# A sandwich layer on one core: attention's small products in halves over two steps, and in another order

## The chip, the cores and the metric

The kernel runs on one core of one Trainium2 chip. The metric is the device time of one execution in microseconds. Before the change it is 2101.61 us, the median of three runs (2100.98 to 2102.13). The profile is one more execution; it took 2102.66 us, of which 2100.9 us lie between its first and its last instruction (the span).

The engines are named as in the profile: PE (matrix products, with PEld for the weight loads that run beside them), DVE (VectorE), ACT (ScalarE), POOL (GpSimd) and SP, which only issues transfers. Each takes its instructions in the order in which the program issues them.

## What is computed

The input x has 8 batches of 512 rows and 512 columns, float32. Two sublayers follow each other, each as x + layernorm(f(layernorm(x))).

```python
# attention, 16 heads of 32 columns; every column is rotated (SPLIT is 0)
c_kv = x @ W_dkv + b_dkv                      # 128 columns
v = c_kv @ W_uv + b_uv
c_q = x @ W_dq + b_dq                         # 128 columns
q = rotary(c_q @ W_qr + b_qr)
k = rotary(x @ W_kr + b_kr)
out = softmax(q @ k.T / sqrt(32)) @ v         # by head
out = out @ W_o + b_o
# feed-forward: two Walsh-Hadamard transforms around a gated layer of 2048
x = fwht(x * SU_ug) / 64
x = silu(x @ W_gate.T * s_g) * (x @ W_up.T * s_u)
x = (fwht(x * SU_dp) / 64) @ W_down.T * s_d
```

The kernel moves the second transform into the down weights: it transforms W_down once, in 16 portions of 32 columns, while attention runs (a "fold"), and writes them to DRAM for the feed-forward part.

## The kernel before

**Steps.** Attention is a loop of 128 steps. Step t belongs to group n = t // 4 and key block c = t % 4; a group is four heads of one batch, so a batch b has 16 steps, i = 0 to 15. What the engines do in a step is written out by hand, in this order:

- `scores_t(n, c)` (L564, L573): transposed scores of one key block of 128 keys for four heads, with the row maximum brought in as a bias by four bf16 products (L564); these mark the start of a step in the trace. ACT exponentiates them in two instructions (L585), the first at once, the second after `bias_rows` where a group ends (c = 3).
- `turn()`: issues pending rotations. A rotation is a DVE shuffle (L420) and three POOL instructions (L421 to L423) which read and overwrite the tile `lin`; `lin` has three buffers.
- `invert` (c = 0), `divide` (c = 3): softmax sums and the quotient.
- `weigh` (L606): probabilities times values, of the key block of the step before.
- `bias_rows(n + 1)` (L550) at c = 3: transposes the row maxima of the next group, which POOL's `split` (L543 to L545) has cut into three bf16 parts.
- `add_up` (L594) at c = 1 and c = 3: four POOL additions that bring two key blocks together. At c = 0 of the next group DVE adds the two pairs (`add_pairs`, L599); `sums` (L623) at c = 2 needs that one.
- a "between" piece, `weighed`, and `row_max` (L527) for the group six steps ahead: scores of 128 queries for four heads, whose maxima DVE takes in two reductions (L535). At c = 1 `split` follows.
- `early`: layer norm and residual instructions on ACT and POOL; a second `turn()`; `later`: statistics, loads and stores; one DVE level of a fold (L493, L494).
- a "behind" piece.

**Pieces.** The projections of the next batch, folds, output projections and input transposes are pieces of work put between these steps by two tables, `BETWEEN` and `BEHIND`, indexed by i. A piece is one to nine products into a PSUM tile of 512 columns and an eviction by ACT: `key` and `compress` four products (3.63 us on PE), `out_proj` five, `query`, `value` and `fold` one (about 1.06 us).

**PSUM.** All pieces, `bias_rows` and `sums` use one bank, `ps_f`, with one buffer. `scores_t` and `row_max` use the three buffers of `ps_s`, four tiles a step: so the second `row_max` tile of a step waits for the first exponential of that step, and the second score tile of the next step waits for a reduction. `wide` puts a piece into `ps_s` instead, so that it may stand next to a piece in `ps_f` (the steps `TWO`).

**Loads and ends.** `load_x` brings the x of the batch after next (1 MB) at i = 4, `x_stats` at i = 6 to 9, `x_norm` at 12, 14, 15 and 0. In the last batch `ENTRY` places the first steps of the feed-forward input (`in_step`) at fixed places. The feed-forward part follows attention and isn't touched.

Of the kernel before, what the change touches and what calls it, by code (L numbers as in the profile page):

```python
# [10 lines left out]
F32 = mybir.dt.float32  # L11
BF16 = mybir.dt.bfloat16
I32 = mybir.dt.int32
AF = mybir.ActivationFunctionType
# [3 lines left out]
P = 128  # L18
NB, S, D = 8, 512, 512
DH, GH = 32, 4  # L20
NK = D // P
NT = S // P
# [11 lines left out]
def sandwich_kernel(  # L34
# [142 lines left out]
    def in_step(j, had, n):  # L177

        if had:
            in_had(j)  # L180
            if j + 2 < n:
                in_shift(j + 2)
            return
        in_flip(j)
        if j + 3 < n:
            in_load(j + 3)
        if j + 1 < n:
            in_norm(j + 1)
        if j + 2 < n:
            in_stats(j + 2)  # L190
# [51 lines left out]
    with ExitStack() as actx:  # L242
# [19 lines left out]
        def load_x(b, by=1):  # L262
            xs[b] = xpool.tile([P, NT, D], F32, tag="x", name=f"x{b}")
            xv = x[b].rearrange("(c p) d -> p c d", p=P)
            for c in range(0, NT, by):
                nc.sync.dma_start(out=xs[b][:, c : c + by, :], in_=xv[:, c : c + by, :])

        def load_row(b, t):

            if b < NB - 1:  # L270
                xr[b, t] = row.tile([P, D], F32, tag="xr", name=f"xr_{b}_{t}", bufs=2)
            else:
                xr[b, t] = fo.tile(
                    [P, D], F32, tag="wwza"[t], name=f"xr_{b}_{t}", bufs=2 - t // 2
                )
            nc.sync.dma_start(out=xr[b, t], in_=x[b, ts(t, P), :])

# [100 lines left out]
        def x_shift(b):  # L378
            mv, rs = stats[b]
            stats[b] = rs, shift_of(mv, rs, NT, f"x{b}")  # L380

        def x_norm(b, t):
            rs, sh = stats[b]
            xn[b, t] = row.tile([P, D], F32, tag="xn", name=f"xn_{b}_{t}", bufs=3)
            nc.scalar.activation(
                xn[b, t], xs[b][:, t, :], AF.Identity, bias=sh[:, t : t + 1], scale=rs[:, t : t + 1]
            )
# [26 lines left out]
        def rotate(dst, ps, bias, scale, name, first=None, second=None):  # L414
            lin = rp.tile([P, S], F32, tag="lin", name=f"lin_{name}")
            nc.scalar.activation(lin, ps, AF.Identity, bias=bias, scale=scale)

            def rest():
                rot = rp.tile([P, S], F32, tag="rot", name=f"rot_{name}", bufs=2)
                nc.vector.stream_shuffle(rot, lin, swap)  # L420
                (first or nc.gpsimd).tensor_mul(lin, lin, cs[:, 0, :])  # L421
                (second or nc.gpsimd).tensor_mul(rot, rot, cs[:, 1, :])
                (first or nc.gpsimd).tensor_add(dst, lin, rot)  # L423

            turns.append(rest)

        turns = []

        def turn():

            while turns:
                turns.pop(0)()

        def key(b, g, wide=False):
            if g == 0:
# [43 lines left out]
            )  # L479
            folds.append((n, w))  # L480

        def fold(n, wide=False):
            _, w = folds.pop(0)
            ps = bank(wide, f"fd_{n}").rearrange("p (c m) -> p c m", c=NI)
            nc.tensor.matmul(ps, lhsT=h128, rhs=w, start=True, stop=True)
            z = fo.tile([P, NI, NF], F32, tag="z", name=f"fz_{n}")
            a = fo.tile([P, NI, NF], F32, tag="a", name=f"fa_{n}")
            nc.scalar.copy(z, ps)

            def level(src, dst, h):  # L490
                sv = src.rearrange("p (a t b) n -> p a t (b n)", t=2, b=h)
                dv = dst.rearrange("p (a t b) n -> p a t (b n)", t=2, b=h)
                nc.vector.tensor_add(dv[:, :, 0, :], sv[:, :, 0, :], sv[:, :, 1, :])  # L493
                nc.vector.tensor_sub(dv[:, :, 1, :], sv[:, :, 0, :], sv[:, :, 1, :])  # L494

            def keep():
                nc.sync.dma_start(
                    out=wdd.rearrange("p (c m) -> p c m", c=NI)[:, :, ts(n, NF)], in_=w
                )

            levels.extend(
                [
                    lambda: level(z, a, 1),
                    lambda: level(a, z, 2),
                    lambda: level(z, a, 4),
                    lambda: level(a, w, 8),
                    keep,
                ]
            )

        levels = []


        brow, nms, pt, o_ps, o_sb, rec = {}, {}, {}, {}, {}, {}
# [245 lines left out]
        for t in range(3):  # L760
# [10 lines left out]

        BETWEEN = {
            0: (x_flip, 1, 1), 1: (x_flip, 1, 2), 4: (x_flip, 1, 3),
            8: (query, 1, 0), 9: (query, 1, 1), 12: (query, 1, 2), 13: (x_flip, 2, 0),
        }
        BEHIND = {
            0: (value, 0, 2), 1: (key, 0, 3), 2: (query, 0, 3), 3: (value, 0, 3),
            5: (compress, 1, "cq"), 6: (key, 1, 0), 7: (out_proj, -1, 0),  # L780
            8: (out_proj, -1, 1), 9: (out_proj, -1, 2), 10: (out_proj, -1, 3),
            11: (key, 1, 1), 12: (compress, 1, "ckv"), 13: (value, 1, 0), 14: (key, 1, 2),
            15: (value, 1, 1),
        }

        FIRST_BETWEEN = {i: p for i, p in BETWEEN.items() if i not in (8, 9)}
        FIRST_BEHIND = {
            **BEHIND, 7: (query, 1, 0), 8: (None, NB, None), 9: (key, 1, 1),
            10: (None, NB, None), 11: (query, 1, 1),
        }  # L790
        OUT = {7: 0, 8: 1, 9: 2, 10: 3}

        APART = {n: (0, 2) for n in range(NG - NK, NG - 2)}
        APART[NG - 2], APART[NG - 1] = (0, 2, 3), (0, 1, 2, 3)

        FOLDS = [4, 10, 15] + [NK * NT * b + i for b in range(1, NB - 1) for i in (4, 10)]
        FOLDS.append(NK * NT * (NB - 1) + 1)
        READ = [0] + [g - 3 for g in FOLDS[1:]]


        TWO = (8, 9, 10, 12, 15)

        def piece(table, b, i, wide=False):
            if b == 0 and table is BEHIND and i == 8:
                out_bias()
            pieces = table if b else FIRST_BETWEEN if table is BETWEEN else FIRST_BEHIND
            if i in pieces:
                fn, d, what = pieces[i]
                if 0 <= b + d < NB:
                    fn(b + d, what, *([True] if wide else []))  # L810
            at = NK * NT * b + i
            if at in FOLDS and (table is BETWEEN) == (b > 0 and i in TWO or i == 15 or b == NB - 1):
                fold(FOLDS.index(at), wide)
            if b == NB - 1 and (i, table is BEHIND) in ENTRY:
                in_step(*ENTRY[i, table is BEHIND], 2 * NT)

        places = [
            (0, False), (4, False), (4, True), (5, True), (6, True), (8, False), (10, False),  # L820
            (11, True), (12, False), (12, True), (13, True), (14, True), (15, True),
        ]
        ENTRY = {place: divmod(s, 2) for s, place in enumerate(places)}
        room["xin"] = lambda name: row.tile([P, D], F32, tag="xn", name=name, bufs=3)
# [9 lines left out]
        def early(b, i):  # L834

            if b > 0 and i - 3 in OUT:
                residual(b - 1, OUT[i - 3])
            if b + 2 < NB and i in (12, 14, 15):
                x_norm(b + 2, max(i - 13, 0))
            if i == 0 and 0 < b + 1 < NB:  # L840
                x_norm(b + 1, 3)

        def later(b, i):

            if b > 0 and i - 1 in OUT:
                out_stats(b - 1, OUT[i - 1])
            if b > 0 and i - 2 in OUT:
                out_shift(b - 1, OUT[i - 2])
            if b > 0 and i - 5 in OUT:
                store(b - 1, OUT[i - 5])  # L850
            if b + 2 < NB:
                if i == 4:
                    load_x(b + 2, NT)
                elif 6 <= i < 10:
                    x_stats(b + 2, i - 6)
                elif i == 11:
                    x_shift(b + 2)

        for t in range(NG * NT):
            n, c = divmod(t, NT)  # L860
# [4 lines left out]
            ends_group = c == NT - 1 and n + 1 < NG  # L865
            if not ends_group:
                second()
            turn()
            if c == 0 and n > 1:
                invert(n - 2)  # L870
            if c == 3 and n > 1:
                divide(n - 2)
            last_steps = t + AHEAD >= NG * NT
            if last_steps:
                piece(BETWEEN, b, i)
            if t > 0:
                weigh(*divmod(t - 1, NT))
            if ends_group:
# [6 lines left out]
                    sums(n - 1, APART[n - 1])  # L885
            elif c == 2 and n > 0:
                sums(n - 1)
            if not last_steps and (i not in TWO or b == NB - 1):
                piece(BETWEEN, b, i)
            if c == 0 and n > 0:  # L890
                weighed(n - 1)
            u = t + AHEAD
# [2 lines left out]
                if u % NT == NT - 1:  # L895
                    split(u // NT)
            early(b, i)
            turn()
            if c == 0 and 0 < n <= NG - NK:
                add_pairs(n - 1)  # L900
            later(b, i)
            if b == 0 and i == 6:
                out_bias_in()
            if levels and (c > 0 or 0 < i and b < 1):
                levels.pop(0)()
            if small:
                small.pop(0)()
            if t in READ:
                fold_load(READ.index(t))
# [14 lines left out]
                load_row(b, i - 12)  # L924
            elif b == NB - 1 and i in (8, 10):
                combine(*units[i // 2 - 4][1:])
            if i in TWO and b < NB - 1:
                piece(BETWEEN, b, i, True)
            piece(BEHIND, b, i)
            if n == NG - 1 and c == 2:  # L930
                invert(NG - 2)

# [682 lines left out]
```

## Time and profile before

| | |
|---|---|
| median of three runs | 2101.61 us |
| profiled execution | 2102.66 us, span 2100.9 us |
| before step 0 | 46.8 us |
| batch 0 | 102.1 us |
| batch 1 | 108.6 us |
| batches 2 to 5 | 108.7 us each |
| batch 6 | 108.1 us |
| batch 7, steps 0 to 12 | 81.6 us |
| from there to the end | 1219.0 us |

The times by batch are differences between the starts of L564 in the timeline. In 257.5 to 366.2 us (batch 2) PE is busy for 108.65 us, DVE 83.71, ACT 57.83 and POOL 90.53. PE's durations in the timeline have modelled ends and overlap; the starts are what is read here. The length of a piece of PE work is therefore the distance from its start to the start of the next one, and a wait shows as a distance that is larger than that of the same work elsewhere. A float32 product shows as two matmul records.

### The profile page before, as it was taken

How to read it: one execution, taken by the hardware profiler on the slowest of the kernel's cores; microseconds unless marked ns; L12 is line 12 of the kernel's file. 1: busy time of each engine (PE TensorE's matmuls, PEld its weight loads, DVE VectorE, ACT ScalarE, POOL GpSimd, SP SyncE). 2: the span in 40 equal slices, each digit the busy share in tenths (PEclk: the TensorE clock that was granted, in tenths of full speed). 3: DMA queues.
4: the chain of work that ended last, by engine and by line, in shares of the span. 5: the costliest groups of instructions: out<-in, count | busy, mean ns of one | idle time of the engine just before them, and what ended most of it. 6: DMA issues, size and time to landing. Idle time of an engine off the chain costs nothing.

```text
span 2100.9 us, 26741 instructions
## 1 busy us (share of the span) xinstructions
PE 2076.8 (99%) x9035; PEld 1057.4 (50%) x9042; DVE 1414.4 (67%) x2356; ACT 745.3 (35%) x1199; POOL 1575.4 (75%) x1629
## 2 busy tenths in 40 slices
PE   8999999999999999999999999999999999999998
PEld 4333333333333333344444677676676766777753
DVE  5698777676767677465545866678866678656542
ACT  3554545555555545522121122222222222222211
POOL 4787979787878889645453678788888879787852
PEclk9999999999999999999999999999999999999999
DMA  3112121212121122237454444444343344444432
GB/s 122 37 31 51 42 54 49 47 51 52 46 57 46 32 66 72 70 104 221 145 166 152 146 143 148 133 138 149 130 157 131 131 137 144 138 158 136 138 112 70
DMA packets 215913, 218.12 MB, mean 104 GB/s; under 512 B 87376, under 2 KB 147920, under 8 KB 215776
## 3 DMA queue, kind: packets, MB, share of 16 engines
q1 hardware_dynamic: 215424, 215.32, 33.2%
q8 instruction: 72, 1.18, 0.2%
q0 software_dynamic: 352, 1.08, 0.1%
q14 instruction: 65, 0.53, 0.1%
HBM read 169.18 MB, written 46.92 MB: 103 GB/s over the span
## 4 chain that ended last, share of the span: by engine, by line
PE 94%; DVE 3%; issue 1%; POOL 1%; ACT 1%; DMA 0%; SPq 0%; POOLq 0%; DVEq 0%; ACTq 0%
PE d L1123 24%; PE psy L1225 18%; PE s L527 6%; PE ops L606 6%; PE ps_k L439 5%; PE ps_y L662 5%; PE t L573 5%; PE u L1106 5%; PE g L1106 4%; PE psz L1516 3%; PE t L564 3%; PE l L623 2%; PE ps_q L454 2%; PE ps_v L466 1%; PE ps_cq L407 1%; PE fxh L207 1%
## 5 line engine op out<-in xcount | busy, mean ns | idle before, releaser
L1225 PE MATMUL psy<-wd,g 128*128 128x512 f32 x896 | 448.9, 592 | 0.0
L535 DVE TENSOR_REDUCE nm<-s 128x2 f32<-128x1024 f32 x256 | 300.8, 1216 | 175.1 <-PE s L527 175.1
L1347 POOL TENSOR_TENSOR pr<-pr,pr 128x512 f32<-128x512 f32 x294 | 391.6, 1357 | 9.0
L594 POOL TENSOR_TENSOR p<-p,p 128x512 f32<-128x512 f32 x244 | 330.2, 1384 | 22.1 <-PE ops L606 22.1
L585 ACT ACTIVATE p<-t 128x1024 f32<-128x1024 f32 x256 | 251.8, 1023 | 89.0 <-PE t L573 89.0
L1123 PE MATMUL d<-xb,wq 128*128 128x256 f32 x992 | 254.2, 380 | 1.9 <-DVE inner L1139 1.4
L1123 PEld LDWEIGHTS d<-tt,wq 128*128 128x128 f32 x864 | 164.0, 190 | 144.4 <-issue 106.0
L1123 PE MATMUL d<-tt,wq 128*128 128x256 f32 x864 | 233.8, 379 | 0.2 <-DVE pr L1144 0.2
L1140 POOL TENSOR_TENSOR pr<-inner 128x256 f32<-128x256 f32 x168 | 126.0, 750 | 138.5 <-DVE inner L1139 105.9
L1123 PEld LDWEIGHTS d<-xb,wq 128*128 128x128 f32 x992 | 186.7, 190 | 62.4 <-issue 30.1
L1225 PEld LDWEIGHTS psy<-wd,g 128*128 128x128 f32 x896 | 169.7, 190 | 49.3 <-issue 29.4
L1136 ACT COPY inner<-d 128x256 f32<-128x256 f32 x168 | 62.6, 373 | 309.6 <-PE d L1123 291.5
L1132 ACT COPY inner<-d 128x256 f32<-128x256 f32 x168 | 62.6, 372 | 300.3 <-PE d L1123 193.2
L527 PE MATMUL s<-kT,qT 32*128 32x512 f32 x1024 | 153.8, 639 | 0.7 <-DVE nm L535 0.7
L573 PE MATMUL t<-qT,kT 32*128 32x512 f32 x1024 | 142.8, 598 | 0.0
L606 PE MATMUL ops<-p,v 128*32 128x512 f32 x1024 | 136.8, 605 | 0.0
L1142 POOL TENSOR_TENSOR pr<-pr,inner 128x256 f32<-128x256 f32 x168 | 136.5, 813 | 0.0
L1123 PE MATMUL d<-T,wq 128*128 128x256 f32 x496 | 127.6, 380 | 0.2
L1144 DVE TENSOR_TENSOR pr<-d,inner 128x256 f32<-128x256 f32 x168 | 70.5, 420 | 75.5 <-PE d L1123 72.9
L439 PE MATMUL ps_k<-xT,wkr_sb 128*128 128x512 f32 x256 | 118.3, 605 | 0.7 <-ACT xT L397 0.7
L662 PE MATMUL ps_y<-wo_sb,oT 128*128 128x512 f32 x256 | 115.8, 593 | 0.9 <-DVE oT L657 0.6
L1135 DVE TENSOR_TENSOR inner<-d,inner 128x256 f32<-128x256 f32 x168 | 70.5, 419 | 62.4 <-PE d L1123 62.0
(219 smaller groups left out, 3263.8 us busy)
## 6 DMA issues: line engine op xcount, KB each, us to landing
wq<-wdeep SPq DMA_DIRECT2D x168, 448.0 KB, 4.2
wd<-wdd SPq DMA_DIRECT2D x112, 256.0 KB, 2.8
wdeep<-w SPq DMA_DIRECT2D x32, 448.0 KB, 5.5
xr<-in_x SPq DMA_DIRECT2D x32, 256.0 KB, 2.8
xin<-x1d SPq DMA_DIRECT2D x32, 256.0 KB, 4.0
xres<-x1d SPq DMA_DIRECT2D x32, 256.0 KB, 3.3
out<-fy SPq DMA_DIRECT2D x32, 256.0 KB, 2.0
rec<-rd SPq DMA_DIRECT2D x124, 64.0 KB, 2.0
```

The lines of the kernel that those rows point to most:

```text
L439: nc.tensor.matmul(ps, lhsT=wkr_sb[:, k, ts(g, P)], rhs=xT[b][:, k, :], start=(k == 0), stop=(k == NK - 1),)
L527: nc.tensor.matmul(sp[j // 2][:, j % 2, :], lhsT=qT[b][rows, g, ts(qc, P)], rhs=kT[b][rows, g, :], start=True, stop=True,)
L535: nc.vector.tensor_reduce(nms[n][:, qc, 2 * h : 2 * h + 2], sp[h], AX.X, ALU.max, negate=True)
L573: nc.tensor.matmul(sp[j // 2][:, j % 2, :], lhsT=kT[b][rows, g, ts(c, P)], rhs=qT[b][rows, g, :], start=False, stop=True,)
L585: nc.scalar.activation(pt[n, c, h], sp[h], AF.Exp)
L594: nc.gpsimd.tensor_add(into, into, pt[n, c, j // 2][:, j % 2, :])
L606: nc.tensor.matmul(o_ps[n][j * DH : (j + 1) * DH, :], lhsT=vv[b][:, c, ds(g * P + j * DH, DH)], rhs=pt[n, c, j // 2][:, j % 2, :], start=( ...
L662: nc.tensor.matmul(ps, lhsT=oT[b][:, k, ts(qc, P)], rhs=wo_sb[:, k, :], start=False, stop=(k == NK - 1),)
L1106: nc.tensor.matmul(ps, lhsT=w[:, SLOT[n], k, :], rhs=rhs[:, k, :], start=k == 0, stop=k == 1)
L1123: nc.tensor.matmul(ps, lhsT=w[:, INNER[m]], rhs=rhs[m], start=True, stop=True)
L1225: nc.tensor.matmul(ys_[t], lhsT=g[:, ts(t, P)], rhs=w, start=n == 0, stop=n == NI - 1)
L1347: nc.gpsimd.tensor_add(pr[n][:, h], pr[a][:, h], pr[b][:, h])
```

## The change

- `halves` puts a small piece (query, value or fold) and a large one (key or compress) together: in one step the first half of the columns of both, in the next step the second. Both halves of a step go into one `ps_f` bank and leave it as two ACT instructions of 256 columns each.
- The two tables become a `plan`. In batches from 1 on: query and key 0 at steps 1 and 2, query 1 and `compress` ckv at 3 and 4, a fold and key 1 at 5 and 6, query and key 2 at 11 and 12, query and key 3 at 13 and 14, a fold and the cq of the batch after next at 15 and 0. The four value pieces stand beside (in `ps_s`, ahead of) the output projections at 7 to 10, the transposes of x at 8, 9, 12 and 13.
- Pending rotations are issued one at a time: ahead of the step's other work only at c = 0 and 2, and at c = 0, 1 and 3 after `add_up` and `split`.
- x is loaded at i = 14 of the batch before, its statistics taken at 1, 2, 3 and 5, its norms at 7, 8, 9 and 11 (other steps in batch 0). Fold loads, folds, the `ENTRY` places and the tiles of the last residual rows move with that; DVE's small instructions for the output bias aren't issued in a step that has a fold level.

```diff
         turns = []
-        def turn():
+        def turn(one=False):
             while turns:
                 turns.pop(0)()
+                if one:
+                    return
...
+        def half(h, ps, fn, b, what):
+            cols = ts(h, HC)
...
+            if fn is query:
...
+                if h == 0:
+                    split_in_two["q"] = rp.tile([P, S], F32, tag="lin", name=f"lin_q{b}_{what}")
+                dst = split_in_two["q"]
+                nc.tensor.matmul(
+                    ps, lhsT=wqr_sb[:, ts(what, P)], rhs=cT[b, "cq"][:, cols], start=True, stop=True
+                )
+                def leave():
+                    nc.scalar.activation(
+                        dst[:, cols], ps, AF.Identity, bias=bqs[:, what : what + 1], scale=QSCALE
+                    )
+                    if h == 1:
+                        rotation(qT[b][:, what, :], dst, f"q{b}_{what}")
+                return leave
+            if fn is key:
...
+                if h == 0:
+                    split_in_two["k"] = rp.tile([P, S], F32, tag="lin", name=f"lin_k{b}_{what}")
+                dst = split_in_two["k"]
...
+            for k in range(NK):
+                nc.tensor.matmul(
+                    ps, lhsT=w[:, k, :], rhs=xT[b][:, k, cols], start=k == 0, stop=k == NK - 1
+                )
...
+        def both(b, i, small_, large):
...
+            if large and small_:
+                for h in range(2):
+                    put(b, i + h, "behind", halves, 0, h, small_, large)
+            elif small_:
+                put(b, i, "behind", *small_)
+        def halves(_, h, small_, large):
+            ps = bank(False, f"ps_{large[0].__name__}_{large[1]}_{large[2]}_{h}")
+            both_ = [(*small_, None, None)[:3], large]
+            for leave in [half(h, ps[:, ts(n, HC)], *which) for n, which in enumerate(both_)]:
+                leave()
...
+        for b in range(1, NB):
+            both(b, 1, (query, b + 1, 0), (key, b + 1, 0))
+            both(b, 3, (query, b + 1, 1), (compress, b + 1, "ckv"))
+            if b < NB - 1:
+                both(b, 5, (fold,), (key, b + 1, 1))
+            for t in range(NT):
+                put(b, 7 + t, "beside", value, b + 1, t)
+                put(b, 7 + t, "behind", out_proj, b - 1, t)
+            both(b, 11, (query, b + 1, 2), (key, b + 1, 2))
+            both(b, 13, (query, b + 1, 3), (key, b + 1, 3))
+            if b < NB - 1:
+                both(b, 15, (fold,), (compress, b + 2, "cq"))
+            for t, i in enumerate((8, 9, 12, 13)):
+                put(b, i, "between", x_flip, b + 2, t)
+        put(NB - 1, 3, "behind", fold)
+        put(NB - 1, 8, "beside", fold)
...
+        NORMS = [(8, 11, 12, 14), (7, 8, 9, 11)]
+        STATS = [(3, 4, 5, 6), (1, 2, 3, 5)]
...
-            turn()
+            if c in (0, 2):
+                turn(True)
...
             early(b, i)
-            turn()
+            if c != 2:
+                turn(True)
...
-            if levels and (c > 0 or 0 < i and b < 1):
+            busy_dve = False
+            if levels and (c > 0 or b == NB - 1):
+                busy_dve = len(levels) % 5 != 1
                 levels.pop(0)()
-            if small:
+            if small and not busy_dve:
                 small.pop(0)()
...
-            if i in TWO and b < NB - 1:
-                piece(BETWEEN, b, i, True)
-            piece(BEHIND, b, i)
+            piece("beside", b, i)
+            piece("behind", b, i)
```

## The prediction, on record before the result was known

> **What bounds the kernel now.** I read the page first (shares, clock, chain of waits), then PE's timeline step by step, then the timelines of POOL and DVE against it.
>
> ```profile
> PE 2076.8 (99%) x9035; PEld 1057.4 (50%) x9042; DVE 1414.4 (67%) x2356; ACT 745.3 (35%) x1199; POOL 1575.4 (75%) x1629
> ...
> PE 94%; DVE 3%; issue 1%; POOL 1%; ACT 1%; DMA 0%; SPq 0%; POOLq 0%; DVEq 0%; ACTq 0%
> ```
>
> PE carries the chain. Its busy share is modelled, so what can be won in attention is read from distances between starts (PE's timeline, batch 5 into 6: start, modelled length):
>
> ```profile
> 683.92 3.70 PE L439 MATMUL ps_k<-xT,wkr_sb 128*128 128x512 f32 x8
> 687.55 0.39 PE L564 MATMUL t<-brow,ones_b 32*128 32x512 bf16 x4
> 687.78 1.02 PE L573 MATMUL t<-qT,kT 32*128 32x512 f32 x8
> 688.74 1.07 PE L606 MATMUL ops<-p,v 128*32 128x512 f32 x8
> ...
> 692.19 0.71 PE L564 MATMUL t<-brow,ones_b 32*128 32x512 bf16 x4
> 692.52 1.24 PE L573 MATMUL t<-qT,kT 32*128 32x512 f32 x8
> 693.70 1.06 PE L606 MATMUL ops<-p,v 128*32 128x512 f32 x8
> ```
>
> After a key piece the transposed scores take 1.19 us (687.55 to 688.74); after a lone value piece 1.51 (692.19 to 693.70). The 0.32 us is the wait for a reduction: too little work stands between `row_max` and the next step's scores. Steps 0, 1, 3, 4, 5 and 14 of a batch have it. This is nearly all that evenly spread pieces can win.
>
> POOL in the same loop works without a pause for long stretches; batch 4, steps 13 to 15:
>
> ```profile
> 568.93 1.28 POOL L421 TENSOR_TENSOR lin_q<-lin_q,cs 128x512 f32<-128x512 f32 x1
> ...
> 572.74 5.32 POOL L594 TENSOR_TENSOR p<-p,p 128x512 f32<-128x512 f32 x4
> 578.01 0.45 POOL L543 CAST parts<-nm 128x16 bf16<-128x16 f32 x1
> ...
> 579.61 1.28 POOL L694 TENSOR_TENSOR y<-xr,y 128x512 f32<-128x512 f32 x1
> 580.85 1.72 POOL L421 TENSOR_TENSOR lin_k<-lin_k,cs 128x512 f32<-128x512 f32 x1
> ```
>
> By starts: a rotation 3.81 us, the four key-block additions 5.27, a split 1.60, a residual 1.24. The rotation stands ahead of the additions here. Two waits of PE in batch 0 show what lateness costs:
>
> ```profile
> 144.98 0.40 PE L550 MATMUL ps_b<-ident_b,parts 128*128 128x128 bf16 x4 [0.68 <-POOL parts L545]
> ...
> 146.98 1.12 PE L485 MATMUL fd<-fw,h 128*128 128x512 f32 x2 [0.53 <-ACT p L585]
> ```
>
> The first is a late split; the second a `ps_s` piece in a c = 3 step, waiting for that step's second exponential.
>
> **The change, part by part.** Basis: the profiled run, 2102.66 us, 1.05 above the median 2101.61; I add the difference to the median.
>
> *Work on PE.* Feed-forward rows show what half columns cost:
>
> ```profile
> 1299.79 1.03 PE L1123 MATMUL d<-xb,wq 128*128 128x256 f32 x4
> 1300.65 1.02 PE L1225 MATMUL psy<-wd,g 128*128 128x512 f32 x2
> 1301.51 0.59 PE L1123 MATMUL d<-tt,wq 128*128 128x256 f32 x2
> ```
>
> Four records of 256 columns take 0.86 us, two of 512 also 0.86: no loss. A half pair is ten such records, 2.15, plus 0.19 of switching (a key piece is 3.63 for 3.44 of records): 2.34 a step, 4.68 for two, against 3.63 + 1.06 = 4.69. The piece moves change nothing but 0.8 us of switching over the whole loop: **-0.8**.
>
> *Batches 1 to 6.* Every step now has at least 2.34 behind it, so the six waits of 0.31 go: -1.86. Waits of `row_max` for the first exponential, 0.91 a batch in steps without anything between (1.22 to 1.33 against 1.07), fall to 4 x 0.18: -0.2. Value beside the output projection at step 7 (c = 3) waits as the fold above: normally `row_max` ends 3.59 into the step, the second exponential at 4.13 in the same ACT rows; with the release +0.63. With small differences -1.2 a batch, six times: **-7**.
>
> *Batch 0.* Its distances hold 7.0 us more than the pieces' own lengths, of which 2.0 at step 0 stay. Afterwards I count 4.2, and 0.7 for late DVE: **-2.2**. The small bias instructions that delayed reductions at step 14 (1.44 on L564) are kept out of fold steps.
>
> *The lin buffers.* `lin` has three buffers. Query 2 and key 2 open two at step 11, query 3 and key 3 two more at step 13; at that moment query 2's rotation is only being issued (step 13, behind `add_up`, `split` and a residual), and key 2's not yet. So one eviction of step 13 must wait until POOL has finished query 2's rotation. From the start of step 13: additions can begin at 2.4 (1.19 + 1.0 + release), +5.27, +1.60, +1.24, +3.81 = 14.3. PE has finished the first half pair at 1.19 + 1.00 + 0.59 + 1.07 + 2.34 = 6.19. ACT stands at the eviction until 14.4, takes it (between 0.37 and 0.69, the rows of 256-column copy and 512-column activation; 0.48, between them for half the columns with a bias) to 14.9, and only then the exponential of step 14 (1.02): 15.9. Queued behind are both exponentials, the copy of `sums` that frees `ps_f`, and so PE's second `row_max` tile and second half pair. Scores end near 16.6, the copy at 17.5, the half pair at 19.9, instead of 6.19 + 6.45 = 12.64: +7.2 a batch, in batches 1 to 6: **+43.4** (batch 6 lacks the transpose, +0.2 there). Bounds: with POOL's shortest rows and nothing contended 6.4; with a late start of POOL 8.0. In the old order such a wait was absent: the tile three before was always rotated several steps earlier.
>
> *DVE, steps 0 to 5.* Shuffles, statistics, fold levels (2.1 us when POOL runs: 0.6 + 1.49) and `add_pairs` (2.4 alone; 4.20 and 2.58 in DVE's timeline at 563.64 and 590.05) sum to 35.9 us against PE's 35.5. Reductions fall behind by up to 2 us; 1.2 of that is covered by the half pair. Between 0 and 1.2 a batch, I take 0.6: **+3.6**.
>
> *Split at step 1 to `bias_rows` at step 3.* Without the lin wait POOL's chain from step 13's additions to that split is 36.9 us against 36.4 on PE, 0.5 late; with the wait PE gives it seven, so 0.
>
> *Batch 7.* The pieces leave its first steps: they get shorter than POOL's and DVE's queues. From step 15 of batch 6 POOL has additions 10.6, two rotations 7.6, input statistics 0.7, split 1.5 and about 2.8 of contention, 23.2; PE reaches `bias_rows` at step 3 after 18.7: 4.5 late. Other waits 5.8 against 6.9 before: **+3.4** (0 to 8).
>
> *Loads.* x (1 MB, 5.4 us to land) and fold portions (3.6) are issued two to three steps, at least 10.7 us, ahead: 0. SP passes nothing it waits for longer than before: the tile of x is free since step 11. Were that cover gone, one load would cost its 5.4.
>
> Sum: -0.8 - 7 - 2.2 + 43.4 + 3.6 + 3.4 = +40.4, so 2142.
>
> [...] PE's gap at step 14 would be some 5.5 us; the longest in this attention loop is 1.27 (on L564 at 134.31, DVE late) and the granted clock 1.00 in every window. [...]
>
> **Rivals.**
> - *No lin wait* (a buffer is free after all; decides if query 2's rotation ends within 6.2 us of step 13's start): then the split at step 1 and the statistics at step 6 are late by 0.6 a batch (+3.5) and batch 7 by 7.7 instead of 4.5: -0.8 - 7 - 2.2 + 3.6 + 3.5 + 6.6 = +4, 2106. For it: nothing in the trace before shows the wait. Against: 14.3 is far from 6.2.
> - *Faster*: no lin wait, and POOL and DVE keep up everywhere, because PE's step lengths become even: -7 - 2.9 - 0.8 - 1.1 = -12, 2090. For it: POOL and DVE idle in steps 7 to 10. Against: both are full in steps 11 to 5.
> - *Slower still*: POOL's additions and rotations run at their contended 1.46 throughout (rows beside DVE's two-input instructions; 1.28 otherwise). The eight instructions ahead of the eviction then end 1.4 later, six times 8.6, and the sixteen of batch 7's chain 2.9: +12 more, 2154. It decides once DVE's fold levels and pair additions fall on them. Against: steps 13 and 14 have no fold level.
> - *It does nothing it says*: the 0.31 waits stay (+11 on any case). Against: steps with a 3.63 piece behind them don't have them, and 2.34 exceeds the 1.4 of a reduction.
>
> **How the numbers follow.** Lin wait 0.72 (2128 to 2158: 6.4 to 8.0 a batch, DVE and batch 7 by their bounds), with POOL slower 0.10 (to 2166, all upper bounds together), no lin wait 0.10, faster 0.08. The range 2120 to 2166 leaves out the last two; its low end takes in a rotation that ends two us earlier than worked out (six times 2 under 2130). A difference under 0.2% (4.2 us) can't be told from none: faster 0.08, same 0.06 (part of the no-wait case), slower 0.86.
>
> **What would show it.** Right: `t` scores 1.19 in steps 0 to 5; half pairs 2.34; in each batch from 1 to 6 an ACT wait of some 7 us on POOL's L423 or its successor before a key eviction at step 13, step 14 about 13 us long, and batches of about 115 us. Wrong: step 14 at 6.5, batches under 109, waits of L550 on POOL at step 3 (no-wait case), or half pairs well over 2.34.

## The result and the profile after

The changed kernel takes 2154.51 us, the median of four runs (2153.49 to 2154.98), beside 2101.77 us of the kernel before on the same chip: a ratio of 1.0251, with a 95% interval from 1.0233 to 1.0269. It is slower by 52.7 us. Its profiled execution took 2154.98 us, with a span of 2153.2.

| by the starts of the bias products of `scores_t` | before | after |
|---|---|---|
| ahead of step 0 | 46.8 us | 45.7 us |
| batch 0 | 102.1 | 104.8 |
| batch 1 | 108.6 | 121.3 |
| batches 2 to 5, each | 108.7 | 116.1 to 116.5 |
| batch 6 | 108.1 | 114.3 |
| batch 7, steps 0 to 12 | 81.7 | 82.4 |
| from there to the end | 1218.9 | 1219.6 |
| step 14 of batches 2 to 5 (within the batches; before, with a whole key piece) | 8.06 | 14.1 to 14.5 |

The page shows PE's share falling, with DVE and POOL taking over parts of the chain that ended last:

```profile
PE 2083.7 (97%) x9452; PEld 1133.6 (53%) x9452; DVE 1408.6 (65%) x2356; ACT 757.3 (35%) x1281; POOL 1566.1 (73%) x1629
...
PE 89%; DVE 5%; POOL 4%; issue 1%; ACT 1%; DMA 0%; SPq 0%; POOLq 0%; DVEq 0%; ACTq 0%
```

The place is one step per batch. PE's timeline of batch 3, from the start of step 14 (start, modelled length; the idle time before an instruction and its releaser in brackets):

```profile
484.30 0.39 PE L646 MATMUL t<-brow,ones_b 32*128 32x512 bf16 x4
...
485.48 1.07 PE L688 MATMUL ops<-p,v 128*32 128x512 f32 x8
492.40 1.93 PE L705 MATMUL l<-p,ones_f 128*32 128x512 f32 x8 [5.85 <-ACT lin_k L589]
494.26 2.05 PE L609 MATMUL s<-kT,qT 32*128 32x512 f32 x8
496.24 0.70 PE L558 MATMUL ps_key<-cq,wqr_sb 128*128 128x256 f32 x2
496.77 1.89 PE L584 MATMUL ps_key<-xT,wkr_sb 128*128 128x256 f32 x8
```

PE stands still for 5.85 us ahead of `sums` (L705), which needs the one buffer of `ps_f`, and ACT has not yet emptied that. ACT's timeline of the same stretch:

```profile
484.40 0.47 ACT L563 ACTIVATE lin_q<-ps_key,bqs 128x256 f32<-128x256 f32 x1 [1.88 <-PE ps_key L584]
491.87 0.47 ACT L589 ACTIVATE lin_k<-ps_key,pv 128x256 f32<-128x256 f32 x1 [6.99 <-POOL qT L426]
492.24 1.93 ACT L667 ACTIVATE p<-t 128x1024 f32<-128x1024 f32 x2
```

The first half of query 3 has its `lin` tile at once; the first half of key 3 waits 6.99 us for POOL's last instruction of query 2's rotation, and both exponentials of step 14 stand behind it. POOL's timeline says why that rotation ends so late:

```profile
480.50 4.95 POOL L676 TENSOR_TENSOR p<-p,p 128x512 f32<-128x512 f32 x4 [2.34 <-PE ops L688]
485.39 0.26 POOL L625 CAST parts<-nm 128x16 bf16<-128x16 f32 x1
...
486.80 1.26 POOL L776 TENSOR_TENSOR y<-xr,y 128x512 f32<-128x512 f32 x1
488.02 1.26 POOL L424 TENSOR_TENSOR lin_q<-lin_q,cs 128x512 f32<-128x512 f32 x1
...
490.58 1.26 POOL L426 TENSOR_TENSOR qT<-lin_q,rot_q 128x512 f32<-128x512 f32 x1
```

Additions, split, residual, rotation, in the order of the prediction. The list of waits has both ends of this chain six times, once in each of batches 1 to 6 (total, times, longest):

```profile
ACT lin_k L589 <- POOL qT L426: 43.3, 6, 8.3
...
PE l L705 <- ACT lin_k L589: 36.5, 6, 7.2
```

Before the change `sums` followed the weighing in step 14 without a gap (PE's timeline, batch 5):

```profile
681.00 1.06 PE L606 MATMUL ops<-p,v 128*32 128x512 f32 x8
681.88 1.04 PE L623 MATMUL l<-p,ones_f 128*32 128x512 f32 x8
682.85 1.14 PE L527 MATMUL s<-kT,qT 32*128 32x512 f32 x8
```

After the standstill `sums` takes 1.86 us from start to start, and `row_max` 1.98; before they took 0.97 and 1.07. The windows of that stretch (after length and busy times: the granted clock, then the share and rate of DMA) show the clock at half from about 489.3 to 496.1 us:

```profile
486.50:489.00 2.50, 0.05 (x4) 0.00 (x0) 0.00 (x0) 0.00 (x0) 2.44 (x4) 1.00 0.00 0
...
489.50:496.00 6.50, 3.60 (x16) 0.72 (x16) 0.00 (x0) 2.89 (x4) 5.99 (x5) 0.50 0.00 0
496.00:496.50 0.50, 0.50 (x5) 0.26 (x2) 0.15 (x1) 0.00 (x0) 0.00 (x0) 0.86 0.05 4
```

What the change was to win is there too. Behind a half pair the scores take 1.19 us (388.22 to 389.41) where a lone value piece left 1.51:

```profile
388.22 0.39 PE L646 MATMUL t<-brow,ones_b 32*128 32x512 bf16 x4
388.45 1.02 PE L655 MATMUL t<-qT,kT 32*128 32x512 f32 x8
389.41 1.06 PE L688 MATMUL ops<-p,v 128*32 128x512 f32 x8
```

A second loss, small in this total but costly later on, lies in steps 1 and 2 of batch 7. PE waits there for reductions:

```profile
857.04 0.39 PE L646 MATMUL t<-brow,ones_b 32*128 32x512 bf16 x2 [1.44 <-DVE nm L617]
...
865.15 0.61 PE L646 MATMUL t<-brow,ones_b 32*128 32x512 bf16 x2 [3.28 <-DVE nm L617]
```

DVE has the pair additions and a fold level ahead of the reduction that the second one waits for:

```profile
858.04 4.19 DVE L681 TENSOR_TENSOR p<-p,p 128x1024 f32<-128x1024 f32 x2
862.15 1.48 DVE L501 TENSOR_TENSOR fa<-fz 128x256 f32<-128x256 f32 x1
863.55 0.41 DVE L502 TENSOR_TENSOR fa<-fz 128x256 f32<-128x256 f32 x1
863.89 2.34 DVE L617 TENSOR_REDUCE nm<-s 128x2 f32<-128x1024 f32 x2
```

### The profile page after: what moved, and what is told of

Same layout as the page of the kernel before. It is cut to its first block, busy times and chain, and to the rows that moved or that the text cites. A ratio compares the mean times of both kernels' runs of the same rounds, so it can differ in the third digit from the quotient of the medians.

```text
span 2153.2 us, 27668 instructions
## 1 busy us (share of the span) xinstructions
PE 2083.7 (97%) x9452; PEld 1133.6 (53%) x9452; DVE 1408.6 (65%) x2356; ACT 757.3 (35%) x1281; POOL 1566.1 (73%) x1629
## 4 chain that ended last, share of the span: by engine, by line
PE 89%; DVE 5%; POOL 4%; issue 1%; ACT 1%; DMA 0%; SPq 0%; POOLq 0%; DVEq 0%; ACTq 0%
PE d L1245 23%; PE psy L1347 18%; PE s L609 5%; PE ops L688 5%; PE ps_y L744 5%; PE g L1228 4%; PE u L1228 4%; PE t L655 4%; PE ps_key L584 4%; PE psz L1638 3%; PE l L705 2%; PE t L646 2%; POOL p L676 2%; PE ps_v L471 1%; DVE nm L617 1%
## 5 line engine op out<-in xcount | busy, mean ns | idle before, releaser
L676 POOL TENSOR_TENSOR p<-p,p 128x512 f32<-128x512 f32 x244 | 315.9, 1326 | 99.8 <-PE ops L688 70.7
L609 PE MATMUL s<-kT,qT 32*128 32x512 f32 x1024 | 159.2, 661 | 0.7 <-DVE nm L617 0.7
L655 PE MATMUL t<-qT,kT 32*128 32x512 f32 x1024 | 137.8, 596 | 0.0
L1282 DVE SCALAR_TENSOR_TENSOR g<-pr,wsu 128x512 f32<-128x512 f32 x96 | 108.9, 1135 | 3.2 <-POOL pr L1469 3.2
```

Source lines behind the costliest of these rows:

```text
L609: nc.tensor.matmul(sp[j // 2][:, j % 2, :], lhsT=qT[b][rows, g, ts(qc, P)], rhs=kT[b][rows, g, :], start=True, stop=True,)
L655: nc.tensor.matmul(sp[j // 2][:, j % 2, :], lhsT=kT[b][rows, g, ts(c, P)], rhs=qT[b][rows, g, :], start=False, stop=True,)
L676: nc.gpsimd.tensor_add(into, into, pt[n, c, j // 2][:, j % 2, :])
```

## Experiments: is it the buffer, the order, or the halves?

Three kernels, each the changed one with one edit.

**Rotation in place.** The eviction goes straight to its place in `qT` or `kT`, and the rotation works there, so no `lin` buffer is needed.

```diff
-            lin = rp.tile([P, S], F32, tag="lin", name=f"lin_{name}")
-            nc.scalar.activation(lin, ps, AF.Identity, bias=bias, scale=scale)
-
-            rotation(dst, lin, name, first, second)
+            nc.scalar.activation(dst, ps, AF.Identity, bias=bias, scale=scale)
+
+            rotation(dst, dst, name, first, second)
...
-                if h == 0:
-                    split_in_two["k"] = rp.tile([P, S], F32, tag="lin", name=f"lin_k{b}_{what}")
-                dst = split_in_two["k"]
+                dst = kT[b][:, what, :]
```

> The evicted query or key goes straight into its place in qT or kT and is rotated there, so no eviction can wait for one of three lin buffers; every instruction and its order are those of the changed kernel. Theory (the fourth lin of step 13 holds up the scalar engine, and through it TensorE, in step 14 of batches 1 to 6; TensorE then runs at half clock for a while): step 14 of these batches falls from 14.1-15.8 us to about 6.5, the sum of their excess is 49 us, so 2154.5 - 49 = 2105.5 us, range 2101 to 2112, with a granted clock of 1.0 throughout. Rival (the wait is one for the late rotation itself, whichever buffer it uses): 2150 to 2156. Rival (halves cost what was lost, spread over all steps): not under 2140.

Measured: 2111.77 us, ratio to before 1.0051 (1.0034 to 1.0068); 42.7 us of the 52.7 are gone. Step 14 of batches 1 to 6 takes 6.46 to 6.47 us. PE's timeline in batch 3:

```profile
469.07 0.39 PE L641 MATMUL t<-brow,ones_b 32*128 32x512 bf16 x4
...
471.13 1.04 PE L700 MATMUL l<-p,ones_f 128*32 128x512 f32 x8
472.11 1.14 PE L604 MATMUL s<-kT,qT 32*128 32x512 f32 x8
473.18 0.70 PE L555 MATMUL ps_key<-cq,wqr_sb 128*128 128x256 f32 x2
```

`sums` follows without a gap and at 0.98 from start to start. So the loss hangs on the buffer, not on the late rotation: that rotation ends 13.8 us after the start of step 13, as late as the 13.7 of the changed kernel, and nobody needs its result yet. The six steps give 48.9 us back by their starts. Some 5.5 us net of that are lost again elsewhere: step 3 of batches 2 to 6 grows from 5.94 to 6.7-6.8 us, and batch 7 from 82.4 to 85.0. In step 3 PE now waits for the split:

```profile
393.69 0.40 PE L627 MATMUL ps_b<-ident_b,parts 128*128 128x128 bf16 x4 [0.80 <-POOL parts L622]
```

This is the wait that the prediction set at 0.5 us for the case without a `lin` wait. In the changed kernel PE's standstill at step 14 let POOL catch up; take it away, and POOL is late. The clock was expected at 1.0 throughout and wasn't in batch 7: in its step 2 PE stands still for 4.71 us until a reduction is done (3.28 in the changed kernel), and the clock is at half for 6.83 us (3.41 there).

**Query 2's rotation ahead of the additions.** Three buffers stay.

```diff
-            if c in (0, 2):
+            if c in (0, 2) or i == 13:
                 turn(True)
```

> Three lin buffers stay; only query 2's rotation is issued at the head of step 13, ahead of add_up, instead of behind it. Theory: the buffer comes free about 4 to 6 us earlier, before the key's first half is evicted, so the wait goes: 2106 us, range 2101 to 2120 (add_up now starts some 2.7 us later, and what it leaves of the wait costs up to 2 us per batch). Rival (four tiles in three buffers cost whatever the order): 2145 to 2156.

Measured: 2114.99 us, ratio 1.0065 (1.005 to 1.008). Step 14 takes 6.46 to 6.47 us in batches 1 to 5; four tiles in three buffers cost nothing there if the oldest is rotated in time. In batch 6 it takes 7.60: ACT still waits 1.83 us for the buffer, and PE 0.68. Step 3 of batches 2 to 6 rises to 7.36-7.47 instead of 6.7-6.8, with PE's wait for the split at 1.36 to 1.47 us: one rotation more stands ahead of POOL's additions.

**The old order of rotations.** All that wait are issued at both places, with halves as changed.

```diff
-            if c in (0, 2):
-                turn(True)
+            turn()
...
-            if c != 2:
-                turn(True)
+            turn()
```

> Rotations in the order before the change: all that wait are issued at both places of every step; three lin buffers, halves and all else as changed. Theory: query 2's and key 2's rotations are issued at the head of step 13, so the lin wait goes here too, but the rotations stand ahead of split and add_up again, which gives back some of the waits of 0.3 us: 2110 us, range 2103 to 2125. Rival (the lin wait depends on the number of tiles alone): 2145 to 2156. Rival (the new order of the rotations is needed by the halves, since two rotations per pair meet on GpSimd at once): slower than 2120.

Measured: 2153.22 us, ratio 1.0246 (1.0231 to 1.0261): no gain. I had expected 2110, and the last rival was right. Step 14 does fall to 6.47 us in batches 1 to 5; ACT waits 0.34 us for the buffer instead of 6.99. The loss has moved, the largest part of it to step 15, 10.5 us instead of 5.94 in batch 3. PE waits 2.88 us there, and the clock is at half for the next 3.41:

```profile
498.10 0.40 PE L632 MATMUL ps_b<-ident_b,parts 128*128 128x128 bf16 x4 [2.88 <-POOL parts L627]
498.43 2.09 PE L609 MATMUL s<-kT,qT 32*128 32x512 f32 x8
```

POOL's timeline: key 2's rotation stands ahead of the additions as well, and PE stands idle until the split behind them has ended.

```profile
487.35 1.29 POOL L424 TENSOR_TENSOR lin_k<-lin_k,cs 128x512 f32<-128x512 f32 x1
...
491.18 4.96 POOL L676 TENSOR_TENSOR p<-p,p 128x512 f32<-128x512 f32 x4
496.07 0.72 POOL L625 CAST parts<-nm 128x16 bf16<-128x16 f32 x1
```

With halves two rotations (7.6 us by the prediction's row) fall due at once. One of them fits ahead of the additions, at the price seen in step 3, two don't, so in these places halves need the new order. Steps 2, 6 and 7 grow as well in this run: in batch 3 PE waits 2.30 and 1.62 us for a reduction of DVE in steps 2 and 6, and 0.85 us for the split in step 7.

## Experiments: the clock, and the order without halves

**PE kept at work through the wait.** In the changed kernel, products of zero weights are added to the open sum `o_ps` where PE would stand.

```diff
             elif c == 2 and n > 0:
+                if 1 <= b < NB - 1 and i == 14:
+                    for _ in range(24):
+                        nc.tensor.matmul(o_ps[n][0:DH, :], lhsT=zero, rhs=bo3, start=False, stop=False)
                 sums(n - 1)
```

> The changed kernel with 24 products of zero weights (0.22 us each by the rows of that shape, 5.3 us together) added to the open sum o_ps ahead of sums in step 14 of batches 1 to 6, so that TensorE works through the wait for lin instead of standing still; the wait itself stays. If a part of the loss is the clock that falls to 0.5 after the standstill (sums 1.86 us instead of 0.97, row_max 2.0 instead of 1.07, half of a query's pieces 0.75 instead of 0.54: 2.0 us a batch): 2154.5 - 12 = 2142 us, range 2139 to 2147, clock 1.0 in all windows. If the longer instructions only fill time that the scalar engine sets anyway: 2152 to 2156.

Measured: 2146.86 us, ratio 1.0216 (1.0201 to 1.0232), 7.6 us less than the changed kernel and not the 12 expected. ACT waits as long as before (43.4 us in six waits for the rotation), but the clock stays up in batches 1 to 5. Windows of batch 3, columns as before:

```profile
484.00:488.80 4.80, 4.10 (x19) 1.65 (x17) 0.00 (x0) 0.52 (x2) 4.72 (x5) 1.00 0.00 0
488.80:493.00 4.20, 4.03 (x25) 2.16 (x26) 2.02 (x2) 2.26 (x3) 3.17 (x3) 1.00 0.01 1
```

Step 14 is 12.78 us there, against 14.1 to 14.9. The slower instructions cost 2.0 us a batch, of which a part was not on the path: with the clock up, the next half pair waits 0.17 us more for ACT's copy of `sums`. In batch 6 the wait is longer; PE's timeline has a standstill of 2.04 us left behind the zero products:

```profile
832.40 1.44 PE L707 MATMUL l<-p,ones_f 128*32 128x512 f32 x8 [2.04 <-ACT lin_k L591]
```

That was enough to lower the clock, by the windows of that stretch:

```profile
830.00:832.40 2.40, 0.36 (x2) 0.00 (x0) 0.00 (x0) 0.52 (x2) 2.32 (x3) 1.00 0.00 0
832.40:838.00 5.60, 5.60 (x25) 2.61 (x26) 2.10 (x2) 2.97 (x4) 3.19 (x3) 0.70 0.03 4
```

So the loss at step 14 divides into 40.6 us of wait (step 14 of this run, 79.4 in all, less 6 x 6.47; a little of batch 6's slow clock is still in it) and some 8 us of clock.

**The new order alone, in the kernel before.**

```diff
-            turn()
+            if c in (0, 2):
+                turn(True)
...
-            turn()
+            if c != 2:
+                turn(True)
```

> The kernel before with the new order of the rotations alone (one at the head of steps c = 0 and 2, one at the end of steps c = 0, 1 and 3). The prediction took some 7 us from the waits of 0.3 us that this order was to remove together with the new places of the pieces: by the order alone 2097 us, range 2094 to 2101. Rival (the order matters only with halves, where two rotations fall due in one step): 2100 to 2103. Rival (a rotation left for a later step makes a lin buffer late here too): over 2108.

Measured: 2117.7 us, ratio 1.0076 (1.0061 to 1.0091), 16 us slower than before. Step 10 of batches 1 to 6 grows from 8.8 to 10.4-10.5 us and step 14 of batch 0 from 9.40 to 14.30; steps 8 and 9 keep their 8.14 and 8.22. None of the expected 4 us came, and the `lin` buffers play no part. The wait is of another kind:

```profile
445.39 1.14 PE L529 MATMUL s<-kT,qT 32*128 32x512 f32 x8 [1.60 <-POOL qT L423]
```

`row_max` of step 10 needs a query whose rotation the slower issue has left over. In the old places of the pieces a rotation had to go out at once. Step 14 of batch 0 is another matter: PE waits 3.87 us there for a reduction that stands in DVE's queue behind the pair additions, a fold level and a small bias operation, and the clock is at half for 6.83 us from 134.4. Together with the old order behind halves (2153 us), this says that places and order of this change belong together, and neither can be priced alone.

## Experiments: what the rest is made of

Without the `lin` wait the kernel is at 2111.8 us, 10 over the kernel before. Four kernels that rotate in place look for these 10 us.

**Three places.** Value behind the output projection at step 7; batch 7's fold levels and folds one step later; the output bias's small operations not held back in batch 0.

```diff
-            piece("beside", b, i)
-            piece("behind", b, i)
+            for place in ("behind", "beside") if i == 7 else ("beside", "behind"):
+                piece(place, b, i)
...
-            if levels and (c > 0 or b == NB - 1):
+            if levels and (c > 0 or b == NB - 1 and i > 0):
...
-            if small and not busy_dve:
+            if small and (b == 0 or not busy_dve):
...
-        put(NB - 1, 3, "behind", fold)
-        put(NB - 1, 8, "beside", fold)
+        put(NB - 1, 4, "behind", fold)
+        put(NB - 1, 9, "beside", fold)
```

> The kernel that rotates in place, with three edits in places that can be read apart: in step 7 of each batch the value projection comes behind the output projection instead of ahead of it (row_max to value 1.67 us in that step, 1.07 in steps 8 to 10: -0.6 us x 6); in batch 7 the fold's levels start one step later and its folds move from steps 3 and 8 to 4 and 9 (step 2 12.4 us, of which 2.8 are two levels ahead of the reduction: -3 to -6 us); the output bias's small operations also run beside fold levels in batch 0 (steps 6 and 7 of batch 1: -1 to -2.9 us). Sum from 2111.8: 2102 us, range 2098 to 2107. If VectorE and GpSimd take each other's time whatever the order: 2107 to 2113.

Measured: 2106.99 us, ratio 1.0023 (1.0014 to 1.0033), at the far end of the range around the 2102 expected. Step 7 gives 0.69 us in each of batches 2 to 6 (8.89 to 8.20). Batch 1's steps 6 and 7 together give 3.6 (18.6 to 15.05). Batch 7's step 2 falls from 12.43 to 8.59, and its step 4 rises from 5.53 to 10.63, so the batch is 1.9 us longer. Step 4 now holds the fold, and it runs at half clock for 6.83 us, behind a standstill of 2.19 us in step 3.

**One addition behind the split.** At c = 1 three of the four additions go ahead of `split`, one behind it.

```diff
-            if c == 1 and n < NG - 1 or c == 3 and n < NG - 2:
+            if c == 1 and n < NG - 1:
+                add_up(n, c, range(GH - 1))
+            if c == 3 and n < NG - 2:
                 add_up(n, c)
...
                     split(u // NT)
+            if c == 1 and n < NG - 1:
+                add_up(n, c, range(GH - 1, GH))
```

> As the kernel of the three edits, with three of the four key-block sums of steps c = 1 ahead of split and the fourth behind it. If GpSimd's queue ahead of split is what bias_rows waits for in step 3 (0.85 us in batches 2 to 6, and 2.5 to 4 us in batch 7's step 2 to 3): 2 to 6 us faster than the three edits alone, so 2098 us, range 2094 to 2103. If VectorE's reduction is what split waits for: within 1 us of the three edits, or up to 4 us slower because GpSimd then stands still ahead of split.

Measured: 2103.77 us, ratio 1.0012 (1.0003 to 1.0021), 3.2 us better than the three edits, but not the 2098 expected. Step 3 is at 5.94 us again, so POOL's queue was what the transposed maxima waited for, and batch 7 is 4.2 us shorter, 2.8 of them in step 4, where the clock now stays up. But step 7 of batches 2 to 5 is back at 8.89 and step 8 rises from 8.54 to 8.89. DVE's timeline at that place in batch 3:

```profile
417.47 1.22 DVE L114 SCALAR_TENSOR_TENSOR sh_x<-mvx,rs_x 128x4 f32<-128x4 f32 x1 [5.00 <-POOL rs_x L105]
418.61 0.68 DVE L734 TENSOR_TENSOR oT<-osb,rec 128x512 f32<-128x512 f32 x1
```

DVE stands 5 us at the shift of x's statistics, which POOL delivers late, with `divide` and a reduction behind it.

**Three attempts on that.** The first puts the fourth addition behind the split in step 1 alone and batch 7's first flat pieces one step later:

```diff
-            (0, False), (1, True), (2, True), (4, False), (4, True),
+            (0, False), (2, True), (3, True), (4, False), (4, True),
```

> The three edits, the fourth key-block sum behind split in step 1 of each batch alone (in step 5 it cost the value's gain in step 7 again: 8.89 us instead of 8.20), and in batch 7 the first two pieces of the flat transposes one step later, since their copy waited 3.5 us for a rot buffer. From 2103.8 us: -0.7 to -1.0 us in steps 7 and 8 of batches 2 to 5 (-4), step 2 of batch 7 8.6 us where 5.2 is free of waits (-1 to -3): 2098 us, range 2094 to 2103, so 0.9965 to 1.0005 of the kernel before. If the pieces of batch 7 only push the reductions of later steps: 2100 to 2106.

The second adds this:

```diff
-            for t, i in enumerate((8, 9, 12, 13)):
+            for t, i in enumerate((9, 10, 12, 13)):
...
-        NORMS = [(8, 11, 12, 14), (7, 8, 9, 11)]
-        STATS = [(3, 4, 5, 6), (1, 2, 3, 5)]
+        NORMS = [(8, 11, 12, 14), (8, 9, 11, 12)]
+        STATS = [(3, 4, 5, 6), (1, 2, 3, 6)]
```

> As the one before it, and the statistics of x's fourth tile move from step 5 to step 6, its norms from steps 7, 8, 9, 11 to 8, 9, 11, 12 and its first two transposes from steps 8, 9 to 9, 10. If the t of step 6 is late by VectorE's work of step 5 (6.85 us in batches 2 to 5, 6.47 in batch 6, where there are no statistics): -0.4 us x 4 to 5, so 2096.5 us, range 2092 to 2102. If step 10, which also has sums, becomes late by the transposes: 2098 to 2106.

The third goes back to the kernel with one addition behind `split` for batch 7 (for the other batches it does so in step 1 alone), gives the copies of the flat pieces a `lin` buffer, keeps the norms of the second, and moves the shift to step 7 with these transposes:

```diff
-            for t, i in enumerate((8, 9, 12, 13)):
+            for t, i in enumerate((9, 11, 12, 13)):
...
-        room["z"] = lambda name: rp.tile([P, S], F32, tag="rot", name=name, bufs=2).rearrange(
-            "p (k q) -> p k q", k=NK
-        )
+        room["z"] = room["flat"]
...
-                elif i == STATS[b > 0][-1] + 1:
+                elif i == 7:
```

> From the kernel with the fourth sum behind split (2103.8 us): in batches 1 to 6 the fourth sum goes behind split in step 1 alone; the shift of x's statistics moves from step 6 to step 7, since VectorE stood 5 us in it for GpSimd's rs_x while the reductions and the divide behind it waited, the norms to steps 8, 9, 11, 12 and the transposes to 9, 11, 12, 13; in batch 7 the copies of the flat pieces take a lin buffer instead of a rot buffer that the last rotations still hold (ACT waited 3.5 us). Steps 7 and 8 of batches 2 to 5 from 8.89 and 8.89 to 8.20 and 8.14, step 11 from 5.94 to 6.53: -0.85 x 4; batch 7 step 2 from 8.6 by -1 to -2. 2099 us, range 2095 to 2104; faster than the kernel before if under 2101. If GpSimd's queue passes each wait on to the next step, as the two kernels before this one did: 2103 to 2108.

| us | rotation in place | three places | one addition behind | first | second | third |
|---|---|---|---|---|---|---|
| median | 2111.77 | 2106.99 | 2103.77 | 2107.51 | 2107.77 | 2103.75 |
| batch 3, step 3 | 6.81 | 6.77 | 5.94 | 5.94 | 5.94 | 5.94 |
| step 7 | 8.89 | 8.20 | 8.89 | 9.07 | 8.40 | 8.40 |
| step 8 | 8.54 | 8.54 | 8.89 | 8.89 | 8.14 | 8.14 |
| step 10 | 8.82 | 8.81 | 8.82 | 8.82 | 10.25 | 8.82 |
| step 11 | 5.94 | 5.94 | 5.94 | 5.94 | 5.94 | 7.27 |
| batches 2 to 5, each | 108.9 to 109.0 | 108.2 | 108.5 | 108.6 | 108.6 | 108.5 |
| batch 7, step 2 | 12.43 | 8.59 | 8.57 | 10.28 | 10.25 | 8.55 |
| batch 7, step 4 | 5.53 | 10.63 | 7.86 | 11.44 | 11.33 | 7.93 |

All three missed their expectations of 2098, 2096.5 and 2099. In the second the transpose at step 10 cost 1.4 us and not only its own 0.6, and step 6, which the statistics of step 5 were thought to delay, stayed at 6.82: that cause is refuted. In the third the transpose at step 11 brought 0.74 us besides its own 0.59: it uses the bank of `bias_rows` and waits until ACT has copied these. Its copies in batch 7 no longer wait for the rotations (3.46 us before), and a wait of 1.43 us ahead of `sums` in step 2 is gone, but the step is as long as before: the scores ahead of it now run at half clock (2.24 us for 1.17), of which more below. Batches 2 to 5 came out between 108.2 and 109.0 us whatever was moved, and the kernel before has 108.7. The best two stand at 1.0012 (1.0003 to 1.0021) and 1.0010 (1.0001 to 1.0019) of the kernel before: level with it, or a hair slower. None beats it.

## Why the prediction was right, and where its terms were off

The forecast was 2142 us in a range from 2120 to 2166; the time is 2154.5. The main case came true. (Its own bounds, 2128 to 2158, are wider than its terms add up to, 2130 to 2155.) The terms one by one, against the spans:

- **The lin buffers (+43.4).** The mechanism is as written: buffer, tile, releasing instruction, the ACT queue behind it, batches 1 to 6. Rotating in place removes it. From the start of step 13 the rotation ends at 13.7 us (478.11 to 491.84) for 14.3 worked out. Without the clock's share the wait costs 40.6 us for 43.4. Two details differ: it surfaces at `sums`, one tile earlier than the second `row_max` tile, because `ps_f` is held by the same late eviction; and it is 6.3 us a step in batches 1 to 5, just under the lower bound of 6.4, and 9.0 in batch 6, where the first of the four additions takes 2.09 us instead of 1.27.
- **The clock (nothing in the sum).** This is the term that was left out, some 8 us of the 12.5 that the forecast fell short by. The trace before had no such standstill to measure, and the sum went by the row with the longest gap, 1.27 us at full clock. In batch 3 of the changed kernel the clock fell 2.76 us after PE had stopped, in a standstill of 5.85, and was at half for 6.83 us; 3.1 of these passed while PE still stood. Shorter standstills lowered it too (last section).
- **The waits of 0.31 and the small terms (-7), late DVE (+3.6).** Scores behind half pairs take 1.19 us, the value at step 7 costs the 0.6 foreseen (1.67 for 1.07). DVE is late by 0.4 us in step 5 and 0.4 in step 6, 0.8 a batch for 0.6. Together batches 2 to 5 would be 0.2 us shorter each if step 14 took the 6.47 us that it takes without the wait; -0.6 was expected. Batch 1 has 2.3 us more than they in steps 6 to 8, which the forecast didn't see: small bias operations run there beside the fold, and the edit in batch 0 that lets them go earlier removes it. None of it comes from the new order alone, which costs 16 us in the old places.
- **Batch 0 (-2.2).** Its work grew by about 6.1 us of pieces from later batches (a key, half a `compress`, a query and two transposes more, one and a half folds less), its time by 2.6: -3.5.
- **Split at step 1 (0 with the lin wait).** Right, and so is what stood beside it: without the wait 0.85 us late in batches 2 to 5 (0.5 worked out).
- **Batch 7 (+3.4).** It has 5.7 us less of pieces and takes 0.8 more, so +6.5, inside the bounds of 0 to 8 but with another place: not the split at step 3 but the reductions behind `add_pairs` (4.19 us for two where it is 2.35 in the same batch before) and a fold level, in steps 1 and 2, with 3.41 us at half clock behind the wait in step 2. The step that failed is "4.5 late" at `bias_rows`: it counted POOL's queue alone, though the DVE row of 2.58 and 4.20 stood in the text.

The rival without a lin wait was put at 2106; the kernel that removes the wait takes 2111.8, with two of the consequences that the rival named: the split late by 0.74 to 0.87 us a batch, and batch 7, the larger one (85.0 us for 81.7 before, with 5.7 us less of pieces, so 9.0, for 6.6). The rival with slower POOL gave nearly the measured 2154 for a wrong reason: in batches 1 to 5 POOL's additions and rotations ran at 1.26 to 1.28 in that stretch, not at 1.46. That the time falls so near it is chance.

## What to carry to other kernels

When pieces are cut in two and paired, count the tiles that are open at once against the buffers of their tag, and write down which queued instruction frees the oldest: an eviction in an in-order queue that waits for a buffer stops everything behind it, here (6.99 us in batch 3) exponentials that had nothing to do with it. A transformation that can be done in its destination needs no such buffer. And when a removed wait leaves less than its size, look for the engine to which the wait had given time: here POOL, about 90 us busy in a batch of 109, was late at step 3 once PE no longer stood still at step 14, and in batch 7 the wait for DVE grew from 3.28 to 4.71 us.

## What was not expected of the hardware

- After a standstill of 5.85 us the clock was at half for 6.83 us (the window of 6.5 us, and 0.19 and 0.14 us by the means of 0.81 and 0.86 in the half microseconds beside it), 3.7 of them after PE had resumed.
- Shorter standstills lowered it too. 2.04 us did (batch 6 of the kernel with zero products: 0.70 over 5.6 us, which is 3.4 us at half), 0.71 us did not. And 1.86 us did it in one kernel and not in another, at the same instruction. PE in step 2 of batch 7, with one addition behind the split:

```profile
812.09 0.39 PE L641 MATMUL t<-brow,ones_b 32*128 32x512 bf16 x2 [1.86 <-DVE nm L612]
812.10 1.24 PE L650 MATMUL t<-qT,kT 32*128 32x512 f32 x8
```

And in the third attempt, where the granted clock is 0.59 from 812 to 816 us (1.00 in the other kernel):

```profile
812.00 0.61 PE L641 MATMUL t<-brow,ones_b 32*128 32x512 bf16 x2 [1.86 <-DVE nm L612]
812.01 2.31 PE L650 MATMUL t<-qT,kT 32*128 32x512 f32 x8
```

In the changed kernel's trace the stretches at half clock within attention last 6.83 us, six of them, or 3.41 us, one, from 864.78. They begin whole multiples of 3.413 us apart: at 257.21, 373.26 and 489.31 us, 34 of them from each to the next. Cut this run into pieces of that length, counted from there. PE stood still for at least 2.36 us in each piece at full clock ahead of a slow stretch, and for at most 1.67 us in every other piece at full clock. (The standstills are by PE's modelled ends.) In the pair above, the clock of the third attempt fell at 811.89 us, and the 3.41 us ahead of that hold 1.74 of the standstill. So in these two traces 1.67 us in a piece did not lower the clock and 1.74 did: the border lies at about half of a piece. In the kernel with one addition behind the split the whole 1.86 us passed at 1.00; that they lay across the end of a piece there is an estimate from these two traces. A difference in batch 7 between two of these kernels is partly the clock.

The same border explains step 14 of the changed kernel, from 14.88 us in batch 1 down to 14.10 in batch 5. PE stops at nearly the same place of the step, and the clock falls 4.04, 3.19, 2.76, 2.50 and 2.36 us later. Of the same 6.83 us at half clock, 5.0 fall on work in batch 1 and 3.3 in batch 5.
